# Attention and mixture of experts in one kernel: the weighting of a step in one piece, and the second half of the next batch's projections due earlier

## The chip, the cores and the metric

The kernel runs on one core of a Trainium2 chip. The metric is device time in microseconds (us) for one launch that does everything, from loading the inputs to storing the output. The core has five engines that each run their own list of instructions in order: the matrix engine (TensorE, PE in the profile), VectorE (DVE), ScalarE (ACT), GpSimd (POOL) and SyncE (SP, which issues most DMAs). They wait for each other by semaphores.

## The reference, cut to what matters

The input `x` has 8 batches of 1024 tokens with 256 features. All data is float32.

```python
x = x + layernorm(attention(layernorm(x)))   # 16 heads of 16 features, causal
x = x + layernorm(moe(layernorm(x)))         # 8 experts, 2 chosen per token

# attention, per batch and head
score = where(causal, q @ k.T / sqrt(16), -inf)
out   = softmax(score) @ v
# moe, per token
gate = min(x @ Wg[e] + bg[e], 7);  up = clip(x @ Wu[e] + bu[e], -7, 7)
y[e] = ((up + 1) * gate * sigmoid(1.702 * gate)) @ Wd[e] + bd[e]
out  = sum over the two best experts of softmax(x @ Wr.T + br)[e] * y[e]
```

## The kernel before

**Two stages.** First comes attention with everything around it, down to the choice of experts for every token; then the expert stage, which works through 71 tiles of 256 tokens of one expert each (`quarter`, L1265 to L1286, and `lower_half`, L1296 to L1306) and puts the outputs back in order (`both`). Between the two, the tokens go through HBM: each token's normalized row is scattered to its two experts' regions by indirect DMAs on the POOL queue (`xsd`, L1044).

**Units.** Attention is cut into 32 units: 8 batches times 4 groups of 4 heads (`b`, `g`). In a unit the four heads lie in the four groups of 32 partitions, so that four small matmuls (32 rows each) run at once, each on its quarter of the rows of the matrix engine. A unit is done in two passes. The first pass (`maxima_tiles`) computes all scores and keeps each query's maximum (`sa`, L686; the maxima on DVE at L696, L702, L711 and L740). The second pass (`values_tiles`), one unit behind, computes the transposed scores once more, this time with the maximum subtracted through an extra row (`sb`, L781), takes their exponentials on ACT (`pT`, L789), masks the diagonal blocks on POOL (L798), and multiplies them with the values (`av`, L818, called the weighting here; it uses the matrix engine as four groups of 32 columns). The row of maxima gets to its place by `rows`: a small reduction (`nm`, L652), a transpose (`nmps`, L655), a copy, and four DMAs on the SP queue (L659).

**Steps and pairs.** A unit has 9 steps. Six hold one row of 512 scores per head (kinds EDGE and WHOLE); three (kind TWO) hold two shorter pieces. A step is done in two pairs: pair 0 computes the scores of heads 0 and 1 of the first pass together with those of heads 2 and 3 of the second pass of the unit before, pair 1 the other way round. Each pair is one group of matmuls with all four row groups at work. The weighting runs two steps late (`DELAY = 2`). After the scores of a pair comes one half of the weighting of step k-2 (`f(kk, half)`), that is 256 of the 512 columns, and then the background (`pump`). In one step of each unit (k = 4, which weights step 2) the two halves belong to two blocks of queries, one of which ends as the other begins: half 0 completes the first block, which DVE must copy out of the single accumulator (`avs`, L829; pool `ps_v`, one buffer) before half 1 can start on the second.

**The background.** Everything else in the attention stage is a list of jobs that are Python generators cut into pieces, each with an estimated cost in us on PE, DVE, ACT and POOL. There are three classes: `urgent` (maxima rows, normalizing of finished rows, masked edges), `due` (the next batch: `prep` normalizes and transposes it, `xps`, L436; `project(b, 0)` and `project(b, 1)` make queries and keys of the first and of the last two units, `pjq` and `pjk`, L591; `values` makes v, `vps`, L577), of which only the first in line may run, and `back` (what follows a finished batch: `finish` with the output projection `aps`, L869, and `yps`, L877, the layer norm and residual; then `route` with the logits, the choice of experts, the slots and the scatters: `x2ps`, L935, `lpsT`, L942, `lps`, L950, `cps`, L996). `pump` adds credit for each engine (at most 0.9 us, 1.3 on POOL) and emits pieces as long as no engine that the piece uses has negative credit. A pair gives PE 0.68 us of credit. The engines' order in attention is exactly this order of emission, for PE, DVE, ACT and SP; POOL's is tied to it by extra dependencies (`in_order`). Jobs of class `back` go on being emitted in the first expert tiles.

**Due times before.** `project(b+1, 0)` is started in the third unit of batch b. `values(b+1)` and `project(b+1, 1)` are started at step 7 of the fourth unit, and forced to an end at the start of the second unit of batch b+1.

**Accumulators.** The scores `sa` have two buffers of two banks each. The scores `sb` and every background matmul share one pool, `ps_b`, of three buffers of one bank, taken in turn; a pair of the second pass takes two of them, each background job at least one. A buffer is free again when ACT or DVE has read it.

Of the kernel before, what the change touches and what calls it, by code (L numbers as in the profile page):

```python
# [58 lines left out]
def attn_moe_kernel(  # L59
# [345 lines left out]
    with ExitStack() as attn:  # L405
# [453 lines left out]

        def finish(b, c):  # L860

            last = b == B - 1
            a = a_toks.pop((b, c)).rearrange("p n h d -> p n (h d)")
            aT = ap2.tile([P, KT, QC], F32, tag="aT", name=f"aT_{b}_{c}")
            for kt in range(KT):
                yield piece(pe=0.5, act=0.6, after=0 if kt else 1)
                ps = ps_b.tile([P, NTB, P], F32, tag="b", name=f"aps_{b}_{c}_{kt}")
                for n in range(NTB):
                    nc.tensor.transpose(ps[:, n, :], a[:, n, ts(kt, P)], ident)  # L869
                nc.scalar.copy(aT[:, kt, :], ps.rearrange("p n q -> p (n q)"))  # L870
            y = ap2.tile([P, NTB, D], F32, tag="y", name=f"y_{b}_{c}")
# [27 lines left out]
            yield from route(b * NC + c, y, last)  # L899
# [18 lines left out]
        def route(t, x1, last):  # L918

            xn = ap2.tile([P, NTB, D + 1], F32, tag="xn2", name=f"xn2_{t}")  # L920
            if last:
                yield from normed(xn, x1)
            else:
                mv, rstd = yield from ln_steps(x1, NTB)
                for n in range(NTB):
                    yield piece(pool=1.25)
                    ln_apply(xn[:, n, :D], x1[:, n, :], mv, rstd, n, nc.gpsimd)

# [149 lines left out]
        def pump(*us):  # L1078

            nonlocal now  # L1080
            for i, more in enumerate(us):
                credit[i] = min(credit[i] + more, 1.3 if i == 3 else 0.9)
            found = True
            while found:
                found = False
                for kind, job in candidates():
                    if job.ready <= now and all(
                        not cost or has >= 0 for cost, has in zip(job.cost, credit)
                    ):
                        for i, cost in enumerate(job.cost):  # L1090
                            credit[i] -= cost
                        emit(kind, job)
                        found = True
                        break
            now += 1

# [21 lines left out]
        with tc.manual_schedule(  # L1118
# [11 lines left out]
            second, late = None, deque()  # L1130
            for u in range(B * NG + 1):
                first = None
                if u < B * NG:
                    b, g = divmod(u, NG)
                    if g == 1:
                        finish_by(jobs["v"], jobs["p1"])
                        if b + 1 < B:
                            jobs["x"] = start(due, prep(b + 1))
                    if g < NG - 1:
                        spread(u + 1)  # L1140
                    if b + 1 < B and g == 2:
                        jobs["p0"] = start(due, project(b + 1, 0))
                    first = maxima_tiles(u)
                for k in range(K):
# [4 lines left out]
                    if first and g == NG - 1 and b + 1 < B and k == K - 2:  # L1149
                        finish_by(jobs["p0"])  # L1150
                        spread(u + 1)
                        jobs["v"] = start(due, values(b + 1))
                        jobs["p1"] = start(due, project(b + 1, 1))
                    for pair in range(2):
# [16 lines left out]
                        halves = (pair,) if first else (0, 1)  # L1171
                        if len(late) > DELAY - 1 or (late and not second):
                            f, kk = late[0]
                            for half in halves:
                                f(kk, half)
                            if 1 in halves:
                                late.popleft()
                        if 1 in halves:
# [5 lines left out]
                        if first and second:  # L1184

                            us = 1.64 + 0.62
                            of_dve = {WHOLE: 1.22, EDGE: 1.68, TWO: 0.72}[STEPS[k][0]]
                            of_act = 1.8 if STEPS[k][0] == TWO else 1.2
                            pump(0.68, us - of_dve, us - of_act, us - 0.35)
# [288 lines left out]
```

## Time and profile before

| what | value |
|---|---|
| time, median of 3 runs | 2270.49 us (2268.22 to 2275.01) |
| profiled execution: its own time, its span | 2275.28 us, 2273.4 us |
| busy: PE, PE's weight loads, DVE | 2195.0, 1363.7, 1627.3 us |
| busy: ACT, POOL | 1091.8, 1070.1 us |
| last weighting of attention | ends about 1435 us |
| first to last expert matmul (L1265) | 1437.1 to 2243.9 us |
| scores `sb`, `sa`: instructions, mean | 3072 of 522 ns, 3072 of 526 ns |
| weighting `av`: instructions, mean | 5120 of 368 ns |

The page counts an engine busy while any instruction of it is under way. Matmuls overlap, and a float32 matmul stands in the profile as two records, so that busy PE time is not the sum of the means. A block of matmuls is best measured from its start to the start of the next block.

### The profile page before, as it was taken

What the parts mean: (1) busy time and instruction counts of PE and PEld (TensorE: products, weight loads), DVE (VectorE), ACT (ScalarE), POOL (GpSimd) and SP (SyncE); (2) the same over time, 40 slices, a digit from 0 to 9 for tenths busy, and PEclk for the clock granted to TensorE, in tenths of its full rate; (3) what the DMA queues carried; (4) which work ended last, traced back from release to release, by engine and by line L of the source; (5) the groups of instructions that cost most, each with busy time, mean ns of one, the idle gap of its engine ahead of it and who ended that gap; (6) DMA issues with size and microseconds to landing.
All of it is one profiled execution on the core that took longest, in us unless ns stands there. A gap on an engine that the chain in (4) does not pass through costs nothing.

```text
span 2273.4 us, 45180 instructions
## 1 busy us (share of the span) xinstructions
PE 2195.0 (97%) x16801; PEld 1363.7 (60%) x16801; DVE 1627.3 (72%) x3677; ACT 1091.8 (48%) x2181; POOL 1070.1 (47%) x1228
## 2 busy tenths in 40 slices
PE   7999999999999999999999999889999999999995
PEld 3444544444444444444445444677888888888884
DVE  4765777777777777777687686665557888887775
ACT  2565665665665666666656656431122323322222
POOL 3321463474364365365365354454444544554543
PEclk9999999999999999999999999999999999999998
DMA  3101102112012013012012010657667877878773
GB/s 81 39 2 39 21 21 58 28 32 58 12 39 48 21 30 86 12 33 55 21 29 58 21 39 30 230 179 221 202 216 256 281 256 268 269 248 279 244 249 110
DMA packets 149106, 251.05 MB, mean 110 GB/s; under 512 B 25920, under 2 KB 111832, under 8 KB 146840
## 3 DMA queue, kind: packets, MB, share of 16 engines
q1 hardware_dynamic: 134168, 210.86, 30.0%
q0 software_dynamic: 12960, 35.47, 4.3%
q8 instruction: 133, 2.18, 0.4%
q10 hardware_dynamic: 1760, 1.84, 0.3%
q14 instruction: 85, 0.70, 0.1%
HBM read 175.66 MB, written 55.68 MB: 102 GB/s over the span
## 4 chain that ended last, share of the span: by engine, by line
PE 83%; DVE 7%; POOL 4%; issue 3%; ACT 1%; DMA 1%; ACTq 0%; POOLq 0%; DVEq 0%; SPq 0%
PE sa L686 19%; PE gu L1265 18%; PE av L818 12%; PE dn L1296 10%; PE sb L781 8%; PE vps L577 3%; PE pjq L591 3%; PE pjk L591 3%; PE yps L877 3%; PE avt L849 1%; PE xtps L1249 1%; POOL pT L798 1%; DVE mx L702 1%; DVE mx L740 1%; DVE sa L696 1%
## 5 line engine op out<-in xcount | busy, mean ns | idle before, releaser
L789 ACT ACTIVATE pT<-sb 128x512 f32<-128x512 f32 x1152 | 625.1, 595 | 348.0 <-PE sb L781 316.8
L781 PE MATMUL sb<-qP,kP 32*128 32x512 f32 (+3 forms) x3072 | 720.0, 522 | 0.5 <-ACT pT L789 0.2
L686 PE MATMUL sa<-kP,qP 32*128 32x512 f32 (+3 forms) x3072 | 657.0, 526 | 6.2 <-DVE mx L702 3.0
L1265 PE MATMUL gu<-xsT,wg 128*128 128x256 f32 x2272 | 520.7, 382 | 2.5 <-ACT xsT L1251 2.5
L1265 PEld LDWEIGHTS gu<-xsT,wg 128*128 128x128 f32 x2272 | 433.9, 191 | 62.8 <-ACT xsT L1251 2.8
L798 POOL TENSOR_SCALAR_AFFINE_SELECT pT<-pT 128x512 f32<-128x512 f32 x256 | 160.3, 642 | 552.8 <-ACT pT L789 368.2
L702 DVE TENSOR_REDUCE mx<-sa 128x2 f32<-128x1024 f32 x256 | 311.5, 1219 | 140.9 <-PE sb L781 137.9
L1276 ACT ACTIVATE sig<-gate 128x256 f32<-128x256 f32 x284 | 118.3, 416 | 569.1 <-DVE gate L1274 540.2
L818 PE MATMUL av<-pT,vpad 128*32 128x256 f32 (+1 forms) x5120 | 366.2, 368 | 1.4 <-DVE avs L829 0.9
L686 PEld LDWEIGHTS sa<-kP,qP 32*128 32x128 f32 x3072 | 229.2, 184 | 207.8 <-issue 133.1
L1281 POOL TENSOR_TENSOR sig<-sig,gate 128x256 f32<-128x256 f32 x284 | 213.4, 753 | 279.8 <-ACT sig L1276 277.7
L781 PEld LDWEIGHTS sb<-qP,kP 32*128 32x128 f32 x3072 | 319.5, 184 | 30.0 <-ACT pT L789 4.6
L818 PEld LDWEIGHTS av<-pT,vpad 128*32 128x32 f32 x5120 | 106.1, 108 | 325.5 <-issue 277.1
L1296 PE MATMUL dn<-wd,act 128*128 128x256 f32 x1136 | 276.2, 384 | 14.1 <-DVE act L1286 14.1
L1274 DVE TENSOR_SCALAR gate<-gu,bs 128x256 f32<-128x256 f32 x284 | 136.0, 479 | 171.6 <-PE gu L1265 156.4
L1296 PEld LDWEIGHTS dn<-wd,act 128*128 128x128 f32 x1136 | 210.8, 192 | 46.5 <-DVE act L1286 21.0
L696 DVE CUSTOM_DVE_ANT_0 sa<-sa,cmask 128x512 f32<-128x512 f32 x256 | 178.3, 696 | 84.4 <-PE sb L781 62.3
L1306 POOL DMA_INDIRECT ytd<-ys,places x142 | 142.6, 1004 | 124.1 <-DVE ys L1302 96.5
L1044 POOL DMA_INDIRECT xsd<-xn,slots x128 | 128.2, 1002 | 107.2 <-DVE xn L1034 46.0
L711 DVE TENSOR_REDUCE mx<-sa 128x2 f32<-128x512 f32 x128 | 88.0, 687 | 88.4 <-PE sb L781 66.1
L1286 DVE SCALAR_TENSOR_TENSOR act<-up,sig 128x256 f32<-128x256 f32 x284 | 124.1, 437 | 21.4 <-POOL sig L1281 21.4
L1278 DVE TENSOR_SCALAR up<-gu,bs 128x256 f32<-128x256 f32 x284 | 134.6, 474 | 0.0
(198 smaller groups left out, 2390.3 us busy)
## 6 DMA issues: line engine op xcount, KB each, us to landing
wg<-_L_ffn_gate_up_proj_dram SPq DMA_DIRECT2D x71, 1024.0 KB
wd<-in_L_ffn_down_proj_dram SPq DMA_DIRECT2D x71, 512.0 KB
xs<-xsd SPq DMA_DIRECT2D x67, 257.0 KB
yy<-ytd SPq DMA_DIRECT2D x16, 1024.0 KB
bs<-biasd SPq DMA_DIRECT2D x71, 132.0 KB
x<-in_L_attn_x_dram SPq DMA_DIRECT2D x16, 512.0 KB
qP<-unq SPq DMA_DIRECT2D x128, 64.0 KB
x1d<-y SPq DMA_DIRECT2D x16, 512.0 KB
```

The source lines that it names most:

```text
L591: nc.tensor.matmul(ps, lhsT=wT[name][:, kt, ts(g2, P)], rhs=xnTs[b][:, kt, ts(c, QC)], start=(kt == 0), stop=(kt == KT - 1),)
L686: nc.tensor.matmul(ps[:, hh, ds(at, w)], lhsT=qP[r, ts(i, P)], rhs=kP[r, ds(c * QC, w)], start=True, stop=True,)
L696: nc.vector.tensor_tensor_reduce(out=ps[:, hh, :], in0=ps[:, hh, :], in1=cmask, scale=1.0, scalar=NEG, op0=ALU.add, op1=ALU.max, accum_out ...
L702: nc.vector.tensor_reduce(mx[:, heads, i, 2:3], ps, AX.X, ALU.max)
L781: nc.tensor.matmul(banks[hh][:, ds(at, QC - off)], lhsT=kP[r, ts(j, P)], rhs=qP[r, ds(c * QC + off, QC - off)], start=True, stop=True,)
L789: nc.scalar.activation(pT[:, 2 * pair + hh, :], banks[hh], AF.Exp)
L798: in_order(nc.gpsimd.affine_select(out=d, in_=d, compare_op=ALU.is_ge, fill=0.0, base=0, pattern=[[0, HG], [1, P]], channel_multiplier=-1,))
L818: nc.tensor.matmul(av[ds(hh * HS, HS), ds(off + a - at, z - a)], lhsT=vp[:, j, ds((g * HG + hh) * VS, HS)], rhs=pT[:, hh, a:z],  start=c n ...
L1265: nc.tensor.matmul(ps[:, half, :], lhsT=wg[:, kt, ds(half * FF + f * P, P)], rhs=xT[:, kt, :], start=(kt == 0), stop=(kt == KT - 1),)
L1281: in_order(nc.gpsimd.tensor_tensor(sg, sg, gt, ALU.mult))
L1296: nc.tensor.matmul(ps[:, n, :], lhsT=act[:, f, ts(n, P)], rhs=wd[:, f, :], start=(f == 0), stop=(f == FT - 1),)
L1306: put = nc.gpsimd.indirect_dma_start(out=yt_dram[:, :], out_offset=bass.IndirectOffsetOnAxis(ap=places[:, i, n : n + 1], axis=0), in_=y[:, ...
```

## The change

A step of attention is emitted as: the scores of pair 0; the background, with the whole step's PE credit (1.36 us); the scores of pair 1; and then the weighting as a whole. Where the background of the step gave less than 1.0 us of PE work, or where the weighted step belongs to two blocks of queries, half 0 of the weighting stays in the middle, now behind the background. At the end of the step a second `pump` adds no PE credit and takes only pieces with at most 0.2 us of PE work. `pump` returns the PE cost that it emitted.

`values(b+1)` and `project(b+1, 1)` are started at the beginning of the fourth unit of batch b instead of at its step 7.

The `finish` and `route` jobs of a block of 512 tokens are held back by a new generator `until`: the output projection of a block waits until the block two before it has its normalized rows for routing, and its routing waits until the block two before it has been routed.

```diff
+        def until(nth, far):
+            while nth >= 0 and gone[nth] < far:
+                yield piece(after=1)
         def finish(b, c):
+            nth = len(gone)
+            gone.append(0)
...
+            yield from until(nth - 2, 1)
             y = ap2.tile([P, NTB, D], F32, tag="y", name=f"y_{b}_{c}")
...
             nc.sync.dma_start(out=x1_dram[b * NC + c], in_=y)
-            yield from route(b * NC + c, y, last)
+            yield from until(nth - 2, 2)
+            yield from route(b * NC + c, y, last, nth)
+            gone[nth] = 2
...
+            gone[nth_job] = 1
...
-        def pump(*us):
+        def pump(*us, most=9.0):
...
-                    if job.ready <= now and all(
+                    if job.ready <= now and job.cost[0] <= most and all(
                         not cost or has >= 0 for cost, has in zip(job.cost, credit)
                     ):
+                        got += job.cost[0]
...
+                    if b + 1 < B and g == NG - 1:
+                        jobs["v"] = start(due, values(b + 1))
+                        jobs["p1"] = start(due, project(b + 1, 1))
...
                         finish_by(jobs["p0"])
                         spread(u + 1)
-                        jobs["v"] = start(due, values(b + 1))
-                        jobs["p1"] = start(due, project(b + 1, 1))
...
-                        halves = (pair,) if first else (0, 1)
+                        us = 1.64 + 0.62
+                        of_dve = {WHOLE: 1.22, EDGE: 1.68, TWO: 0.72}[STEPS[k][0]]
+                        of_act = 1.8 if STEPS[k][0] == TWO else 1.2
+                        left = us - of_dve, us - of_act, us - 0.35
+                        middle = first and pair == 0
+                        got = pump(1.36, *left) if middle and second else 0.0
                         if len(late) > DELAY - 1 or (late and not second):
                             f, kk = late[0]
+                            if middle:
+                                apart_of = len({t[0] for t in STEPS[kk][2]}) > 1
+                                halves = (0,) if got < 1.0 or apart_of else ()
+                                begun_with = halves
+                            else:
+                                halves = tuple(
+                                    h for h in range(2) if not (first and h in begun_with)
+                                )
                             for half in halves:
                                 f(kk, half)
-                            if 1 in halves:
+                            if not middle:
                                 late.popleft()
...
                         if first and second:
-                            us = 1.64 + 0.62
-                            of_dve = {WHOLE: 1.22, EDGE: 1.68, TWO: 0.72}[STEPS[k][0]]
-                            of_act = 1.8 if STEPS[k][0] == TWO else 1.2
-                            pump(0.68, us - of_dve, us - of_act, us - 0.35)
+                            if not middle:
+                                pump(0.0, *left, most=0.2)
```

More of the change, by code (lines that the diff above doesn't have):

```diff
@@ L858, in normalize @@
                 start(back, finish(b, c))
+        gone = []
+        def until(nth, far):
+            while nth >= 0 and gone[nth] < far:
+                yield piece(after=1)
         def finish(b, c):
+            nth = len(gone)
+            gone.append(0)
             last = b == B - 1
@@ L916, in normed, with route @@
             yield piece(after=1)
-        def route(t, x1, last):
+        def route(t, x1, last, nth_job):
             xn = ap2.tile([P, NTB, D + 1], F32, tag="xn2", name=f"xn2_{t}")
@@ L1076, in candidates @@
                     yield (due if kind is not urgent and kind is not back else kind), job
-        def pump(*us):
+        def pump(*us, most=9.0):
             nonlocal now
+            got = 0.0
             for i, more in enumerate(us):
@@ L1095, in pump @@
             now += 1
+            return got
         def finish_by(*jobs):
@@ L1129, in attn_moe_kernel @@
             jobs["p1"] = start(due, project(0, 1))
-            second, late = None, deque()
+            second, late, begun_with = None, deque(), ()
             for u in range(B * NG + 1):
@@ L1170, in attn_moe_kernel @@
                             use()
-                        halves = (pair,) if first else (0, 1)
+                        us = 1.64 + 0.62
[4 more added lines that the diff above has]
+                        got = pump(1.36, *left) if middle and second else 0.0
                         if len(late) > DELAY - 1 or (late and not second):
                             f, kk = late[0]
+                            if middle:
[6 more added lines that the diff above has]
+                                )
                             for half in halves:
                                 f(kk, half)
-                            if 1 in halves:
+                            if not middle:
                                 late.popleft()
-                        if 1 in halves:
+                        if not middle:
                             if first:
@@ L1184, in attn_moe_kernel @@
                         if first and second:
-                            us = 1.64 + 0.62
-                            of_dve = {WHOLE: 1.22, EDGE: 1.68, TWO: 0.72}[STEPS[k][0]]
-                            of_act = 1.8 if STEPS[k][0] == TWO else 1.2
-                            pump(0.68, us - of_dve, us - of_act, us - 0.35)
+                            if not middle:
+                                pump(0.0, *left, most=0.2)
                         elif first:
```

## The prediction

> **What bounds the kernel now.** I read the page's slices first, then the chain that ended last by engine, then PE's timeline. From the page:
>
> ```profile
> PE 2195.0 (97%) x16801; PEld 1363.7 (60%) x16801; DVE 1627.3 (72%) x3677; ACT 1091.8 (48%) x2181; POOL 1070.1 (47%) x1228
> ...
> PE   7999999999999999999999999889999999999995
> ...
> PE 83%; DVE 7%; POOL 4%; issue 3%; ACT 1%; DMA 1%; ACTq 0%; POOLq 0%; DVEq 0%; SPq 0%
> ```
>
> PE carries 83% of the chain and is busy almost throughout, also in attention (slices 2 to 25). That doesn't say that it works at its peak. The timeline of PE shows how its time is made up (start, duration, line, tile, shape, count):
>
> ```profile
> 616.00 0.66 PE L869 MATMUL aps<-ident,atok 128*128 128x128 f32 x4
> 616.58 0.70 PE L686 MATMUL sa<-kP,qP 32*128 32x512 f32 x2
> ...
> 617.65 0.64 PE L818 MATMUL av<-pT,vpad 128*32 128x256 f32 x8
> 618.22 1.99 PE L877 MATMUL yps<-woT,aT 128*128 128x256 f32 x8
> 620.15 0.70 PE L686 MATMUL sa<-kP,qP 32*128 32x512 f32 x2
> ```
>
> From start to start: a pair's scores (S) 1.07 us, half a weighting (A) 0.57, an output projection 1.93. Two halves in a row occur in the last unit:
>
> ```profile
> 1430.06 1.07 PE L818 MATMUL av<-pT,vpad 128*32 128x256 f32 x16
> 1431.06 1.99 PE L877 MATMUL yps<-woT,aT 128*128 128x256 f32 x8
> 1432.98 1.94 PE L818 MATMUL av<-pT,vpad 128*32 128x256 f32 x32
> ```
>
> They take 1.00 us, not 2 x 0.57: each change of kind costs about 0.14 us behind an A. A background block (B) before an A costs the same 1.92 as before S. Scores with background right behind them, as the changed order has them, stand in the first unit:
>
> ```profile
> 58.40 1.13 PE L686 MATMUL sa<-kP,qP 32*128 32x512 f32 x4
> 59.46 1.98 PE L591 MATMUL pjk<-xnT,wkT 128*128 128x512 f32 x4
> ```
>
> 1.06 us, so that order has no price of its own. I cut PE's timeline from 80 to 1425 us into S, A and B blocks. Above their shortest forms, about 100 us are waits: 79 inside S (for the `sb` buffers, mostly), the rest behind A and B.
>
> **What the Trainium skill says.** "TensorEngine Tiling (Array Packing)", Key Properties: changing the tiling mode drains the TensorE, changing the tile within a mode doesn't. The trace agrees: 0.57 + 0.57 against 1.00. "Perfetto Trace Analysis", Identifying the Most-Contended Engine: matmul busy time is no measure of headroom, weight loads are a better one. It agrees: in attention the loads are busy 75 to 77 of each 160 us while matmuls show 159. "PSUM — Partial Sum Buffer", Specifications: eight banks. The pools take 4 + 3 + 1, so the three `ps_b` buffers can't simply be more; the waits in S are its sign in the trace.
>
> **The change, part by part.** The built order of the changed kernel, between first and last weighting, against that of before: S 562 and 562; A blocks 564 and 418; B blocks 284 and 233. So 155 steps have their weighting whole; the others keep a half in the middle.
>
> 1. *Fewer drains at A*: 146 x 0.14 = 20.4 us gained.
>
> 2. *Fewer drains at B*: a normalizing transpose and a key projection together take 2.30, apart 0.59 + 1.91 = 2.50; two transposes together 1.02, apart 1.17. So 51 x 0.17 = 8.7 gained.
>
> 3. *Scores behind half a weighting alone.* Before, 275 S come 0.57 us after the last S and wait 0.15 on average (41 in total): the third `ps_b` buffer is free, the next one only when the exponential (0.595) of the last pair is read, 0.72 after its scores. After the change 181 are left, 27 us; the 148 S behind a whole weighting have 1.00 us of cover and should wait for nothing. Gain 14.
>
> 4. *Lost cover.* With no A in the middle, S1 comes right behind B. With one background job it needs both exponentials, about 1.22 us (a single transpose job, 1.17 after S, waits 0.05). With two, B's first job holds the buffer that S1 wants, and ACT reads it behind the exponentials. The chain of waits before shows it with an A as cover:
>
> ```profile
> 317.31 0.57 PE av L818 x8
> 317.88 1.02 PE x2ps L935 x8
> 318.90 0.63 PE sa L686 x2
> ...
> 320.26 0.57 PE av L818 x8
> ```
>
> S lasts 1.36, 0.29 over; so two jobs need 1.9 after S (2.1 in TWO steps, where ACT also copies edges, 0.59). Projections (1.92) and longer need no cover. But 43 packs of two or three short jobs, about 1.0 us long, just reach the 1.0 that moves A away: 43 x 0.9 = 39 us. B followed by A (78) keeps its cover, 21. Sum 60 against 44 by the same rule before (the trace has 53): 16 lost.
>
> 5. *The step that is split between two blocks.* DVE's copy `avs` (0.69) was queued right behind the first maxima; now up to 1.5 us of background pieces stand ahead of it on DVE, and only one S (1.07) lies between its two halves. Half 1 queues behind it on PE, and everything else behind that. From the order, in about nine of 31 units such pieces meet no or short background: 0.9 to 1.2 us each, 8 lost. Bounds 0 and 20.
>
> 6. *The earlier due time* adds and removes nothing: the same matmuls and ACT copies, no DMA, spread over two units instead of one; no lump at a forced end stood in the order before, so I take 0. Its cover is the slack of ACT (62% busy here); without it, seven batches' 56 copies x 0.59 = 33 us of ACT would meet the exponentials, as they do now.
>
> 7. *The hold-back and the tail.* Back jobs get PE credit only once per step and wait for each other. In the built order one routing more (block 13: `x2ps` 8 matmuls, `lpsT` 8, `lps` 1; 1.8 us of PE, moved, not saved) falls into the expert stage. Its layer norm (4 x 1.23 on POOL) stands in front of the gate products (L1281) there; its scatters were in that stage before as well. Windows there:
>
> ```profile
> 1435.00:1480.00 45.00, 36.25 (x166) 30.52 (x167) 32.80 (x105) 16.13 (x32) 25.32 (x28) 0.92 0.76 265
> 1480.00:1520.00 40.00, 37.44 (x215) 31.26 (x214) 31.23 (x110) 15.95 (x31) 23.09 (x26) 1.00 0.55 187
> 1520.00:1560.00 40.00, 32.58 (x127) 26.41 (x126) 18.89 (x55) 4.69 (x11) 20.31 (x23) 0.83 0.69 200
> ```
>
> PE (second figure) is not full: the first eight expert tiles take 122.6 us, against 10.8 each later, 36 over. An added exponential there swaps ACT's tables twice (1.28 each, as the trace has them). I take 5 lost, bounds 0 and 15. The second expert table is now emitted in tile 9 instead of 7; tile 12 needs it, two tiles (21.6 us) later, so loads stay covered.
>
> Sum: -20.4 - 8.7 - 14 + 16 + 8 + 5 = -14 us. Against the profiled execution's 2275.3 that is 2261; that one lies 4.8 above the median of the runs, so I forecast 2256 for the median.
>
> **Rivals.** (a) *The tail takes it*: three routings in the thin stage between the two instead of two and a bit; at 36 us for what is there, a third at 12 and a later table bring the gain to about nothing, 2268. For it: POOL waits and scatters on the chain there. Against: they are now spread over ten tiles, not eight. (b) *The lost cover decides* (slower): place, S1 behind 86 packs of two or three jobs without an A. I take 0 for the long ones and 0.9 for the short. If ACT or DVE reads a pack's first job late also there (edge copies, a DVE queue with 1.2 us maxima), by 0.55 each, that is 47 us: 2303; it turns the sign from 14/86 = 0.16 us on. A nearer value is 2285. Against: before, long packs (2.89 us behind S) waited 0.0 to 0.1. (c) *More gain*: items 4, 5 and 7 cost nothing, since S1 is late only where S0' would have been: -29 - 14 = -43, 2227; half of that, 2238, is likelier. (d) That it isn't done in full: true for 126 steps and already counted.
>
> **How the numbers follow.** My forecast 0.50 (2244 to 2264), (a) 0.20 (2262 to 2276), (b) 0.14 (2278 to 2303), (c) 0.16 (2227 to 2244). 0.3% is 6.8 us, about what a measurement can tell from no change: below 2263.7 lie nearly all of the forecast, (c) and a little of (a), 0.67; within, 0.19; above 2277.3, 0.14. The range 2234 to 2279 leaves out half of (c) and most of (b); the likeliest case's own is 2244 to 2264.
>
> **What would show it.** Right: `av` blocks of 16 records at 1.00 us, about 155 of them; S behind them at 1.07; S behind packs of two short jobs at 1.9 to 2.0; attention ending 15 to 25 us earlier; the first ten expert tiles 5 us longer in sum. Wrong: waits of S behind projections (b), or `avs` waits over 1 us in every unit; expert tiles 0 to 9 more than 15 us longer (a); fewer waits inside S in total than the 79 us of before (c).

## The result, and the profile after

| | before | after |
|---|---|---|
| time, median of the runs (us) | 2272.75 (2268.2 to 2277.9) | 2342.95 (2335.8 to 2348.0) |
| ratio | 1 | 1.0306, interval 1.0269 to 1.0343 |
| span of the profiled execution | 2273.4 | 2342.4 |
| first expert matmul | 1437.1 | 1464.5 |
| the first ten expert tiles together | 144.2 | 185.7 |
| from the eleventh tile to the start of the last | 652.5 | 652.5 |

The forecast was 2256 with a range of 2234 to 2279. The kernel became 70 us slower, and the loss has two places: 27.4 us in attention and 41.5 us in the first ten expert tiles. Together they are the 69.0 us by which the spans differ.

From the page after (busy times, PE by slice, the chain by engine):

```profile
PE 2188.7 (93%) x16801; PEld 1360.2 (58%) x16801; DVE 1631.4 (70%) x3677; ACT 1090.9 (47%) x2183; POOL 1071.0 (46%) x1228
...
PE   7999999999999999999999989776999999999995
...
PE 81%; DVE 6%; POOL 4%; ACT 4%; issue 4%; DMA 2%; ACTq 0%; POOLq 0%; SPq 0%; DVEq 0%
```

PE is busy for 6.3 us less, with the same 16801 matmul records, and the span is 69 us longer. The hole in the slices has grown from "889" to "89776". That is the tail; the 27 us in attention don't show here, since a slice of 58 us is still a "9" with 1 us more of waiting in it.

The windows of the tail after (columns: stretch, its length, then busy time and instruction count of PE, PEld, DVE, ACT and POOL, PE's granted clock, DMA share, GB/s):

```profile
1465.00:1510.00 45.00, 31.82 (x154) 24.77 (x153) 18.04 (x55) 13.81 (x26) 21.54 (x22) 0.85 0.57 195
1510.00:1550.00 40.00, 27.73 (x121) 22.72 (x120) 20.77 (x71) 9.10 (x20) 20.43 (x23) 0.83 0.51 164
1550.00:1590.00 40.00, 34.35 (x170) 28.77 (x173) 26.61 (x85) 11.83 (x24) 15.42 (x18) 0.87 0.39 132
```

PE, DVE and POOL all do less than in the same stage before, where PE had 36 of 45 and 37 of 40 us. No engine is full, so they wait for each other or for a transfer.

**Attention, cut into blocks.** PE's timeline between the first weighting and the last, cut as in the prediction into scores (S), weightings (A) and background (B): "shortest form" is what the blocks would take at the durations that the prediction used, "above it" is the rest.

| us | before: shortest form | above it | after: shortest form | above it |
|---|---|---|---|---|
| S | 601.3 | 79.0 | 601.3 | 84.3 |
| A | 326.6 | 15.2 | 306.2 | 7.0 |
| B | 322.9 | 10.5 | 312.8 | **71.2** |

The saved changes of kind are there in number: 30.5 us at the prediction's prices. What takes them, and 27 more, is 61 us of waits inside background. By the number of jobs (each fills one `ps_b` buffer) in a block that stands right behind scores:

| jobs in the block | blocks | wait inside, each | sum |
|---|---|---|---|
| 1 | 109 | 0.02 us | 2.0 us |
| 2 | 98 | 0.53 us | 52.0 us |
| 3 | 17 | 0.92 us | 15.6 us |

One of them in the timeline after (start, duration, engine, line, what, and in brackets how long the engine had been idle and who ended that):

```profile
659.16 0.59 PE L686 MATMUL sa<-kP,qP 32*128 32x512 f32 x2
659.18 0.59 PE L781 MATMUL sb<-qP,kP 32*128 32x512 f32 x2
...
659.70 0.28 PE L655 MATMUL nmps<-ident,nm 128*16 128x128 f32 x1
...
659.93 1.09 ACT L789 ACTIVATE pT<-sb 128x512 f32<-128x512 f32 x2 [0.80 <-PE sb L781]
...
660.58 0.65 PE L849 MATMUL avt<-ident,avs 128*128 128x128 f32 x4 [0.60 <-ACT pT L789]
660.90 0.24 ACT L657 COPY nmT<-nmps 16x128 f32<-16x128 f32 x1
...
661.07 1.98 PE L591 MATMUL pjk<-xnT,wkT 128*128 128x512 f32 x4
...
662.98 0.70 PE L686 MATMUL sa<-kP,qP 32*128 32x512 f32 x2
```

The pair's scores have taken two of the three `ps_b` buffers, and `nmps`, the pack's first job, takes the third. The second job, `avt`, has to take over the buffer that the first exponential reads. That exponential begins at 659.93, takes 0.60, and `avt` starts at 660.58. The third job, `pjk`, gets the buffer of the second exponential, which is read until 661.02, and starts at 661.07. That is 0.49 us behind `avt`, a distance that it also has in e5 below with half a weighting ahead, so nearly all of the loss lies in front of the second job. The pack takes 3.28 us; its shortest forms add up to 2.36. Before the change half a weighting (0.57 us) stood between scores and pack, and most of the first exponential's time passed under it. In the list of PE's waits of attention before, background waits for the exponentials come to 1.0 us; after, the list begins with

```profile
PE avt L849 <- ACT pT L789: 9.9, 20, 0.6
PE x2ps L947 <- ACT pT L789: 7.6, 18, 0.6
PE yps L886 <- ACT pT L789: 5.5, 14, 0.5
```

(us in all, times, longest), and so on through twelve kinds of job; the weight loads (PEld) show more of the same.

**The tail.** POOL's waits from 1430 to 1660 us, the row that has changed, first of before, then of after (us in all, times, longest):

```profile
POOL xsd L1044 <- DMA xn<-second: 11.0, 2, 6.8
```

```profile
POOL xsd L1056 <- DMA xn<-second: 35.7, 4, 12.1
```

`xsd` are the scatters; those for a token's second expert need new row numbers in the rows' last column, and a small DMA on SP's queue writes these (`xn<-second`). The last of the four waits, in the timeline after:

```profile
1620.08 0.37 SPq L1259 DMA_DIRECT2D wg<-_L_ffn_gate_up_proj_dram  x1
...
1621.24 0.37 SPq L1267 DMA_DIRECT2D wd<-in_L_ffn_down_proj_dram  x1
...
1623.45 0.61 SPq L1052 DMA_DIRECT2D xn<-second  x1
...
1637.08 0.96 POOL L1056 DMA_INDIRECT xsd<-xn,slots  x1 [12.06 <-DMA xn<-second]
...
1639.33 0.73 POOL L1311 TENSOR_TENSOR sig<-sig,gate 128x256 f32<-128x256 f32 x1
1640.09 0.42 DVE L1316 SCALAR_TENSOR_TENSOR act<-up,sig 128x256 f32<-128x256 f32 x1 [14.72 <-POOL sig L1311]
...
1640.57 1.22 PE L1326 MATMUL dn<-wd,act 128*128 128x256 f32 x2 [13.37 <-DVE act L1316]
```

The write of 2 KB is issued 3.4 us behind an expert's 1 MB and 2.2 us behind its 512 KB. POOL stands at the scatter until 1637. The gate product `sig` is queued behind the scatters, DVE stands at `act` for 14.7 us, and PE at `dn` for 13.4. (In this last of the four, ACT had itself been held by another DMA until 1632.9; POOL's wait outlasts that by 4 us.)

Why the write comes late is not the same each time. The four writes were ready 5.9, 2.8, 7.6 and 13.6 us after their issue; in the first two cases POOL had stood for 3.5 and 4.0 us before the write was issued at all, and seven DMAs of zeros (257 KB each, L262) are issued 1.7 us behind the last one. Whether the bulk loads ahead of it hold the write back was not tested.

One remark on the numbers below: the kernel before takes 2274 us on the chip of the runs e1 to e4, but 2291 and 2292 on the two chips of e5 to e8 and e9 to e12, where attention with the order of before is some 25 us longer (1461.9 against 1437.1 for the first expert matmul; two single waits inside scores of 4.0 and 4.8 us are part of it). Times are therefore set against the kernel before on the same chip, and attention against a kernel with the same order on the same chip; the forecasts of the first expert matmul for e5 to e12, made from 1437 and 1464, have to be read in this way. e1 to e9 are one execution each. The first scores start between 25.9 and 32.7 us, before any of the edits can act, and shift the first expert matmul with them; so the table also has the time from the first weighting to the last.

### The profile page after: what moved, and what is told of

It reads as the page before. It is cut to its first block, busy times and chain, and to the rows that moved or that the text cites. A ratio compares the mean times of both kernels' runs of the same rounds, so it can differ in the third digit from the quotient of the medians.

```text
span 2342.4 us, 45151 instructions
## 1 busy us (share of the span) xinstructions
PE 2188.7 (93%) x16801; PEld 1360.2 (58%) x16801; DVE 1631.4 (70%) x3677; ACT 1090.9 (47%) x2183; POOL 1071.0 (46%) x1228
## 3 DMA queue, kind: packets, MB, share of 16 engines
q1 hardware_dynamic: 134168, 210.86, 29.2%
## 4 chain that ended last, share of the span: by engine, by line
PE 81%; DVE 6%; POOL 4%; ACT 4%; issue 4%; DMA 2%; ACTq 0%; POOLq 0%; SPq 0%; DVEq 0%
PE sa L686 20%; PE gu L1295 18%; PE av L818 11%; PE dn L1326 9%; PE sb L781 7%; ACT pT L789 3%; PE vps L577 3%; PE pjk L591 3%; PE pjq L591 3%; PE yps L886 2%; PE xtps L1279 1%; POOL xsd L1056 1%; PE avt L849 1%; PE x2ps L947 1%; DMA xn<-second 1%
## 5 line engine op out<-in xcount | busy, mean ns | idle before, releaser
L781 PE MATMUL sb<-qP,kP 32*128 32x512 f32 (+3 forms) x3072 | 710.3, 523 | 1.9 <-ACT pT L789 1.0
L818 PE MATMUL av<-pT,vpad 128*32 128x256 f32 (+1 forms) x5120 | 336.6, 366 | 5.0 <-DVE avs L829 5.0
L781 PEld LDWEIGHTS sb<-qP,kP 32*128 32x128 f32 x3072 | 293.7, 184 | 43.2 <-ACT pT L789 6.7
L1326 PE MATMUL dn<-wd,act 128*128 128x256 f32 x1136 | 276.6, 384 | 32.7 <-DVE act L1316 32.7
L818 PEld LDWEIGHTS av<-pT,vpad 128*32 128x32 f32 x5120 | 121.1, 109 | 238.5 <-issue 176.4
```

Source lines behind the costliest of these rows:

```text
L781: nc.tensor.matmul(banks[hh][:, ds(at, QC - off)], lhsT=kP[r, ts(j, P)], rhs=qP[r, ds(c * QC + off, QC - off)], start=True, stop=True,)
L818: nc.tensor.matmul(av[ds(hh * HS, HS), ds(off + a - at, z - a)], lhsT=vp[:, j, ds((g * HG + hh) * VS, HS)], rhs=pT[:, hh, a:z],  start=c n ...
L1326: nc.tensor.matmul(ps[:, n, :], lhsT=act[:, f, ts(n, P)], rhs=wd[:, f, :], start=(f == 0), stop=(f == FT - 1),)
```

## The experiments

The theories at the start. **Theory 1**: attention loses because the second and third job right behind scores wait for the buffers that the exponentials read. Its rivals: the larger lumps of background cost by themselves, or the earlier due time does. **Theory 2**: the tail loses because one more block is routed there, and its scatters wait for late writes. Its rivals: the order of the step spoils the tail itself, or the routing's own work fills it.

All runs in one table (us; "second scatters" is the sum of POOL's waits for `xn<-second` in the expert stage):

| kernel | first expert matmul | first to last weighting | waits in S | in B | ten tiles | second scatters | time | before, same chip |
|---|---|---|---|---|---|---|---|---|
| before | 1437.1 | 1352.8 | 79 | 11 | 144.2 | 11.0 | 2272.8 | |
| after | 1464.5 | 1380.1 | 84 | 71 | 185.7 | 35.7 | 2343.0 | 2272.8 |
| e1 old order, due + hold | 1454.6 | 1370.2 | 99 | 12 | 137.7 | 5.0 | 2286.2 | 2274.3 |
| e2 new order alone | 1478.3 | 1393.6 | 99 | 68 | 141.9 | 11.0 | 2313.8 | 2274.3 |
| e3 new order + hold | 1474.6 | 1389.4 | 99 | 66 | 155.3 | 15.5 | 2323.9 | 2274.3 |
| e4 before, swapped | 1480.9 | 1394.5 | 95 | 52 | 158.1 | 5.7 | 2332.6 | 2274.3 |
| e5 before, lumps behind half 0 | 1469.8 | 1390.5 | 128 | 15 | 141.5 | 11.7 | 2304.9 | 2290.9 |
| e6 after, one job behind scores | 1461.3 | 1381.3 | 118 | 4 | 186.0 | 36.7 | 2341.3 | 2290.9 |
| e7 after, late scatters | 1488.2 | 1403.1 | 107 | 69 | 141.7 | 3.8 | 2323.0 | 2290.9 |
| e8 before, late scatters | 1461.9 | 1373.9 | 97 | 13 | 138.4 | 0 | 2293.9 | 2290.9 |
| e9 after, half exponentials | 1439.9 | 1356.9 | 75 | 49 | 185.3 | 31.5 | 2319.1 | 2291.8 |
| e10 = e6 + e7 | 1458.4 | 1378.2 | 117 | 3 | 141.3 | 3.2 | 2297.0 | 2291.8 |
| e11 before, long single jobs ahead | 1453.3 | 1369.0 | 98 | 13 | 140.2 | 0 | 2284.0 | 2291.8 |
| e12 as e11, whole step's credit | 1466.1 | 1381.0 | 121 | 21 | 140.4 | 0 | 2297.8 | 2291.8 |

### Which part of the change loses (e1 to e3)

e1 takes the new order of the step out and keeps the rest:

```diff
-                        middle = first and pair == 0
-                        got = pump(1.36, *left) if middle and second else 0.0
+                        halves = (pair,) if first else (0, 1)
 ...
+                            pump(0.68, us - of_dve, us - of_act, us - 0.35)
```

> The order of the step undone (half, scores, half, background as before); the earlier due time and the hold-back stay. Theory 1 (background right behind the scores waits for the score buffers) expects the loss in attention gone: first expert matmul at 1437 +-5 us, as before. Theory 2 (the tail is lost to the routing of block 13, moved into the expert stage, and to the scatters there) expects the first ten expert tiles at 144 +-10 us, since only blocks 14 and 15 are routed there in this order; time about 2275. Rival: the earlier due time or the hold-back carry the loss; then this run lies 20 us or more over the kernel before.

Measured: 12 us over the kernel before; first expert matmul 17.5 us later, ten tiles 6.5 us shorter. Background waits are gone (12 us), as Theory 1 says. But attention is not back: waits inside scores grew from 79 to 99. So the earlier due time and the hold-back together are not free in this order, which neither theory had; the two were not taken apart here. The rival, 20 us or more in all, did not come either. By the unit's place in its batch (first to fourth, sums over eight batches), background in shortest form and waits inside scores:

| us | before: B, waits in S | e1: B, waits in S | e2: B, waits in S | after: B, waits in S |
|---|---|---|---|---|
| first units | 96, 17 | 85, 23 | 108, 15 | 73, 18 |
| second | 90, 18 | 56, 33 | 69, 40 | 74, 25 |
| third | 81, 19 | 75, 22 | 81, 17 | 73, 24 |
| fourth | 56, 25 | 108, 21 | 57, 27 | 93, 18 |

The early due time moves v and second projections into the fourth unit and leaves the second nearly bare, and there the waits of e1 are largest. In each pair of columns they are largest where the unit has least background, or nearly least. That is a pattern and no proof, and in the second units of e2 something else stands behind it. Of their 40 us, 12 are five single waits of 1.9 to 3.1 us, one in each batch from the third to the seventh, behind a pack of `avt` and `x2ps` or `aps`. One of them in e2's timeline:

```profile
598.67 0.65 PE L849 MATMUL avt<-ident,avs 128*128 128x128 f32 x4
...
599.53 0.66 PE L945 MATMUL x2ps<-ident,xn 128*128 128x128 f32 x4 [0.20 <-ACT pT L789]
...
601.52 0.42 DVE L853 TENSOR_TENSOR atok<-avt,rec 128x256 f32<-128x256 f32 x1
...
602.10 0.66 PE L781 MATMUL sb<-qP,kP 32*128 32x256 f32 x1 [1.28 <-DVE atok L853]
```

DVE reads `avt` only behind several small steps of the routing and a maximum, and the second `sb` of the next pair waits for that buffer. Before the change no wait inside scores is longer than 1.2 us.

e2 takes out the two other edits instead; e3 takes out only the earlier due time:

```diff
-            yield from until(nth - 2, 1)          # e2 only
-            yield from until(nth - 2, 2)          # e2 only
-                    if b + 1 < B and g == NG - 1:
-                        jobs["v"] = start(due, values(b + 1))
-                        jobs["p1"] = start(due, project(b + 1, 1))
 ...
                         spread(u + 1)
+                        jobs["v"] = start(due, values(b + 1))
+                        jobs["p1"] = start(due, project(b + 1, 1))
```

> The new order of the step alone, without the earlier due time and without the hold-back. Theory 1: attention as long as after the change or a little longer (in the built order 91 blocks of two and 21 of three jobs come right behind scores, against 98 and 17), first expert matmul at 1464 to 1470 us. Theory 2: routing of blocks 14 and 15 only in the expert stage, so its first ten tiles take 144 +-10 us and the time is about 2300. Rival to theory 2 (the order of the step spoils the tail itself): ten tiles at about 186 us, time about 2343. Rival to theory 1 (the earlier due time costs the attention's 27 us): first expert matmul at 1437 or before.

> The new order of the step with the hold-back, the earlier due time alone undone. Theory 1: attention as after the change, first expert matmul at 1464 +-5 us. Theory 2: block 13 is routed in the expert stage here too, so the ten tiles take 186 +-12 us and the time is about 2343. Rival (the earlier due time carries part of the loss): 15 us or more less than after the change.

Measured, adding one edit at a time:

| | attention | ten tiles |
|---|---|---|
| new order of the step (e2 less before) | +41.2 | -2.3 |
| hold-back (e3 less e2) | -3.7 | +13.4 |
| earlier due time (after less e3) | -10.1 | +30.4 |
| sum | +27.4 | +41.5 |

The order alone loses more in attention than I expected (1478, not 1464 to 1470): background waits as priced (68 against 48 + 19 = 67 by Theory 1's prices), and 20 us more inside scores than before the change. Nine waits of over 1.4 us make 18.5 of these 20, the five above among them. With the new order the earlier due time gives 10 us back: the five waits are gone (waits of over 1.4 us: 18.0 us in e3, 5.0 after). In e3 the five packs stand in step 2 of the second units, and DVE is done with `avt` 3.3 to 3.5 us after its start; after the change such packs stand in step 5 of the first units, DVE is done after 1.7 to 2.0 us, and the scores wait 0.6. So it has no sign of its own. The -2.3 and -3.7 of the table say nothing, since four executions of the kernel before differ by up to 9.7 us. The tail's part of Theory 2 was right for e2 (141.9). It missed for e3: block 13 is routed in the expert stage there too, and the ten tiles took 155, not 186 +-12. So the extra routing isn't the size of the loss. What goes with it is the column of second scatters: 11.0 us of waits in e2, 15.5 in e3, 35.7 after. Nor does one edit make the loss of the tail: in e1 the due time and the hold-back without the order leave 137.7 us. The new order with the earlier due time but without the hold-back was not run.

### Behind the scores, or lumps anywhere (e4 to e6)

e4 is the kernel before with the two statements of a pair exchanged: `pump` ahead of `f(kk, half)`. Every instruction of before is there, but part of the output comes out wrong in this order; why was not traced, and only the times of its attention are used.

> The kernel before with one edit: in each of a step's pairs the background is put ahead of the half weighting, so that it comes right behind the scores; no weighting is whole, no hold-back, the old due time. In the built order 194 background blocks of one job come right behind scores, 78 of two and 5 of three. Theory 1 prices them at 0, 0.53 and 0.92 us: 46 us lost, 6 saved by fewer and longer blocks; first expert matmul at about 1470 us. Rival (the loss comes from the whole weighting, or from uneven load on ACT and DVE, not from what stands behind the scores): at 1437 or a little before.

Measured: 1480.9, more than the 1470 expected; background waits 52 us, 0.51 in front of two jobs and 0.65 of three, against 0.53 and 0.92 priced, and 16 more inside scores. So no whole weighting and no lump of a whole step is needed for the waits; to stand right behind scores is enough.

e5 makes the lumps without putting them behind scores:

```diff
-                            pump(0.68, us - of_dve, us - of_act, us - 0.35)
+                            if pair:
+                                pump(0.0, *left, most=0.2)
+                            else:
+                                pump(1.36, *left)
```

> The kernel before with one edit: the whole step's background is given in the step's first pair, behind half 0 of the weighting (as in the kernel before, a weighting stands between the scores and it), and the second pair gets next to none. As large lumps as after the change (118 blocks of one job, 93 of two, 22 of three), but none right behind scores. Theory 1 (what counts is that the lumps stand right behind scores) expects no loss: first expert matmul at 1437 - 9 (fewer changes of kind) = 1428 +-6 us. Rival (the lumps themselves cost, wherever they stand): 1455 us or more. The tail at 144 +-15 us.

Measured: from the first weighting to the last 16.6 us longer than e8, whose attention is that of the kernel before on the same chip. (The first expert matmul is only 7.9 us later, because e5's first weighting starts 8.7 us sooner.) Theory 1 in this form wanted 9 less, the rival at least 18 more; both miss, the rival by little. The waits inside background stay away (15 us against e8's 13). The same three jobs as in the timeline above, here behind half a weighting:

```profile
646.85 0.64 PE L818 MATMUL av<-pT,vpad 128*32 128x256 f32 x8
647.42 0.28 PE L655 MATMUL nmps<-ident,nm 128*16 128x128 f32 x1
647.63 0.66 PE L849 MATMUL avt<-ident,avs 128*128 128x128 f32 x4
648.12 1.98 PE L591 MATMUL pjk<-xnT,wkT 128*128 128x512 f32 x4
650.03 0.70 PE L686 MATMUL sa<-kP,qP 32*128 32x512 f32 x2
```

From `nmps` to the next scores 2.61 us, against 3.28. But the lumps do cost, in another place: scores behind them wait 66.7 us (232 times) against 49.6 (283 times) in e8, and those with only half a weighting ahead 61.7 (329) against 47.6 (279), 31 us more inside scores in all. The mean behind lumps, 0.29 us, is not the price of every lump: the median is below 0.01. Fifteen waits of over 1.4 us make 31.6 us of the total, against four and 12.0 in e8; five of them (11.4 us) stand behind `avt` with `x2ps` or `aps` as in e2 above, four (10.7 us) behind `lpsT`. So there are two prices: one inside a pack that stands right behind scores, paid by nearly every such pack, and one in the next scores for a step's background in one lump, paid mostly in a few places that come back with each batch.

e6 is the changed kernel with at most one PE job behind the scores; more of them go behind half 0:

```diff
-                        got = pump(1.36, *left) if middle and second else 0.0
+                        got = pump(1.36, *left, jobs=1, tick=0) if middle and second else 0.0
 ...
-                                halves = (0,) if got < 1.0 or apart_of else ()
+                                halves = (0,) if got < 1.0 or apart_of or more_to_do() else ()
 ...
+                        if middle and second:
+                            pump(0.0, 0.0, 0.0, 0.0)
```

> The changed kernel with one edit: at most one PE job goes right behind the scores; where more are due, half 0 of the weighting follows it and the others stand behind that (224 blocks of one job right behind scores, none of two or three; built nominal length 1252 against 1220). Theory 1: waits inside background 0.02 each instead of 0.53 and 0.92, so 67 us less waiting against 32 us more changes of kind: first expert matmul at 1437 +-8 us. Rival (the waits come from the load on ACT and DVE and only move): 1464 us or later, the waits then inside the scores. The tail as after the change, 186 +-15 us.

Measured, from the first weighting to the last: 21.8 us less than e7, which has the changed kernel's attention on the same chip, and 7.4 more than e8. (The first expert matmul flatters e6 by the 5.0 and 7.9 us that its first weighting starts sooner.) Between e8 and e7 lie 29.2 us, so three quarters of the loss in attention are gone. Background waits fall by 64 us, scores wait 11 more, and 32 us of changes of kind come back: the sum is -21 by the blocks. The 7.4 that remain are 21 us more inside scores than in e8 against 14.5 less in weightings. The tail is unchanged at 186, as expected.

### The second scatters (e7 and e8)

```diff
-                    yield piece(after=(2 if last else 1))
+                    yield piece(after=(8 if t >= NT - LATE else 1))
```

> The changed kernel with one edit: for the last four blocks the second expert's scatters are emitted eight ticks of the background pump behind the write of their row numbers, instead of one or two, so that POOL's queue goes on with gate products while that write is on its way. Attention as after the change (1464 +-4 us). Theory 2 (POOL stands at the second scatter for that write, 36 us in all in the expert stage, and the gate products behind it stop DVE and PE): ten tiles 20 to 35 us shorter than 186 us. Rival (the routing's own work on PE, DVE and POOL fills the stage): within 8 us of 186.

> The same edit on the kernel before. Attention at 1437 +-3 us. Its trace shows 11 us of waits at the second scatter in the expert stage (4.2 and 6.8), so Theory 2 expects ten tiles of 144 - 11 = 133 +-6 us and a time of about 2263. Rival: 144 +-4 us, no change.

Measured: ten tiles 141.7 in e7, 44 less than after the change and than e6 on the same chip, more than the 20 to 35 expected and all of the tail's loss; 138.4 in e8, 5.8 less than before and 3.1 less than e5 on the same chip (133 +-6 was expected). e8's forecast of 11 us less in all did not come: one execution took 2293.9 us against 2290.9 for one of the kernel before, and single executions can't tell a few us (46 of the kernel before on the chip of e9 to e12 lie between 2286 and 2303). What is left of the four waits in e7, from POOL's list of waits of the stage (us, times, longest):

```profile
POOL xsd L1056 <- DMA xn<-second: 3.8, 1, 3.8
```

And from PE's list, the wait for `act`, after the change and in e7:

```profile
PE dn L1326 <- DVE act L1316: 29.3, 6, 13.4
```

```profile
PE dn L1326 <- DVE act L1316: 2.9, 3, 1.5
```

Block 13 is routed in the expert stage in e7 too. So it is the wait that costs and not the work, and Theory 2 stands in that narrower form. The 24.7 us of such waits more than before come with 41.5 us of time. One part of the rest is on record: after the change the granted clock of PE was 0.83 to 0.87 in all four windows of the ten tiles (1465 to 1650 us), in e7 1.00, 0.87, 1.00 and 1.00 (1488 to 1630), and PE was busy for 135.6 us there against 126.1. The lower clock goes along with the waits; how the rest comes about was not taken apart. e4's 158 us with only 5.7 us of such waits is not explained by this and stays open.

### The wait measured by its cause (e9)

```diff
-                        nc.scalar.activation(pT[:, 2 * pair + hh, :], banks[hh], AF.Exp)
+                        nc.scalar.activation(
+                            pT[:, 2 * pair + hh, : QC // 2], banks[hh][:, : QC // 2], AF.Exp
+                        )
```

> The changed kernel with exponentials of half the columns (128x256; POOL fills the other half of each weighting tile with ones, so the attention's values are not the reference's); the order on PE is unchanged. An activation of 128x256 takes 0.42 us in the gate's row, one of 128x512 0.60: 0.18 less. Theory 1 (the second job right behind the scores waits for the end of the first exponential, the third for that of the second) expects 0.53 - 0.18 = 0.35 us in front of two jobs and 0.92 - 0.36 = 0.56 in front of three: 44 us instead of 68 in all inside the background. Rival (the wait is the background's own: its inputs, its own reads by ACT and DVE, or changes of kind): 0.53 and 0.92 as before.

Measured: 0.37 us in front of two jobs (98 blocks) and 0.58 in front of three (17), 47 us in all. The exponential's end sets the wait in front of the second job: 0.16 us less where its time is 0.18 less. The rival is out. The 0.58 for three jobs agrees with 0.56 in the sum but not in the parts: in `nmps`, `avt`, `pjk` (seven times) the second job starts 0.66 us behind the first instead of 0.88, and the third 0.49 behind the second in both kernels. So the second exponential is at most a small part of the 0.92.

### Both causes, and what is left as gain (e10 to e12)

> Both suspected causes taken out of the changed kernel together: one PE job at most right behind scores (as in the kernel with cover), and the late second scatters. Theory 1 and Theory 2 together expect attention at 1437 +-8 us and ten tiles at 141 +-6 us, that is the time of the kernel before, 0.997 to 1.005 of it. Rival (a third cause): over 1.008.

Measured: 1.0025 of the kernel before, interval 1.0015 to 1.0035. The two edits bring 3.1% down to a quarter of a per cent; no third cause of size is left in the sum. It is a sum, though: scores still wait 117 us, and fewer changes of kind pay for that.

e11 is the kernel before, with the late scatters, and with a long job alone ahead of half 0:

```diff
+                        long_one = middle and second and next_is_long(*spare)
+                        if long_one:
+                            pump(*spare)
 ...
+                                begun_with = (0,) if not long_one or apart_of else ()
 ...
-                            pump(0.68, us - of_dve, us - of_act, us - 0.35)
+                            if not long_one:
+                                pump(*spare)
```

> The kernel before with what the runs left as gain: in a step's first pair, where the next PE job is a long one (1.0 us or more), it stands alone ahead of half 0, and the weighting follows whole behind the second scores; everywhere else the order and the credit of each pair are those of before; the late second scatters added. In the built order 34 weightings are whole and 41 single jobs stand right behind scores. Theory 1: 34 x 0.14 = 4.7 us gained, no new waits inside the background; Theory 2: ten tiles at 138 instead of 144. Sum -11: 0.993 to 0.998 of the kernel before. Rival (any background right behind scores costs more than it saves): 1.000 or above.

Measured: 0.9967 of the kernel before, interval 0.9952 to 0.9982, faster than both kernels. Its blocks against e8's (on another chip): waits inside scores 98 and 97, inside background 13 and 13, weightings 336.7 us against 342.2. The 5.5 us are the 34 changes of kind (4.7 expected); the 41 jobs right behind scores wait 0.03 us each.

e12 does the same with the whole step's credit in the first pair (`pump(0.0, *left)` behind a credit of 1.36).

> As the last, but with the changed kernel's credit: the step's whole background in its first pair, ahead of half 0 if its first PE job is a long one, behind it otherwise (60 blocks of one job and 6 of two right behind scores, 65 weightings whole, 233 blocks in all; built nominal length 1233 against 1250.8). Theory 1 in its first form: 18 us gained, 3 lost, attention at 1422 us. What the kernel with lumps behind half 0 showed (waits inside scores of 0.29 us each behind lumps, about 25 us in all) says the gain is eaten: 1437 +-8 us. Ten tiles at 138 +-5 us; time 0.990 of before by the first, 0.996 to 1.001 by the second.

Measured: 1.0022 of the kernel before, interval 1.0010 to 1.0034, just above the second forecast and far from the first. Scores behind background wait 0.29 us on average (231 times, 67 us), the figure of e5, and as there it is made in a few places: waits of over 1.4 us inside scores are 18 with 33.4 us, against 4 with 14.2 in e11, and these 19 us are most of the 23 that e12's scores wait longer. What the long jobs gain is lost there.

## Why the prediction was wrong

**Steps 1 and 2, fewer changes of kind: right.** 29.1 forecast, 30.5 by the number of blocks in the trace (A 20.4, B 10.1), at the same prices. The price for A holds when measured on its own: 5.5 us for 34 in e11.

**Step 3, scores behind half a weighting alone: wrong in size.** A gain of 14 was forecast. The 148 scores behind a whole weighting wait 0.03 each, as it said; but the 182 others wait 0.22 instead of 0.15, so that all together wait 45 us against 41 before. There is no gain. Why the others wait longer was not tested.

**Step 4, lost cover: this is the step that failed in attention.** It asked how long the scores *behind* a pack wait: nothing behind the 43 long packs, 39 us behind the 43 short ones. The long ones came as said (2 us), the short ones cost 16. It did not ask how long the pack itself waits, and said "Projections (1.92) and longer need no cover". They do not cover their own start: `avt` + `pjq` takes 2.77 us behind scores where 1.92 and 0.4 were due. 16 us of loss were forecast at the scores behind background, where 3 came (39 against 36); what came besides was 68 us inside packs, where the second job waits for the buffer that the first exponential reads. The evidence for the order was misread. The first-unit example (scores, then `pjk`, 1.06 us) was taken as a sign that this order "has no price of its own". But those scores are `sa` alone: no `sb` holds a `ps_b` buffer there, no exponential reads one, and a single job stands behind. And all packs of before that were looked at had half a weighting ahead of them, which is the cover whose price was asked for.

**Step 5, the split step: right in size.** 8 forecast; waits in the scores between its two halves grew by about 7.

**Step 6, earlier due time at 0: wrong, with no sign of its own.** With the hold-back 17.5 us later in e1's order, alone 10.1 earlier in the changed one. The step counted matmuls and copies, which are the same, and not what stands next to what: in the changed order the earlier due time moves the packs of `avt` and `x2ps` or `aps`, which held up the scores in e3, to a step where DVE reads `avt` sooner. What it does in e1's order is open.

**Step 7, the tail: wrong by the largest amount.** 5 forecast, bounds 0 and 15; measured 41.5. The step counted the moved routing's work and said that "its scatters were in that stage before as well". It left out that each second scatter waits for a DMA on SP's queue and stops all of POOL's work behind it: 35.7 us of such waits against 11.0. With the late scatters the same routing costs nothing (e7).

**The rivals.** (b) had the right kind, "lost cover", and 0.55 us each; it put it in the scores behind the pack, and against it stood the long packs of before, which were covered. What it describes, DVE reading a pack's first job late, does occur in e2 and e3, but five times, for 12 us, and not after the change. That its 2303 is near what the order alone gives (2314 in e2) is therefore luck. (a) named POOL's waits in the tail, but with 12 us. Neither alone reaches 2343; both came together.

Of its own signs, the 155 whole weightings at 1.00 us and the scores at 1.07 behind them came as said. "S behind packs of two short jobs at 1.9 to 2.0" did not (short packs: 1.45 on average), nor did "attention ending 15 to 25 us earlier" and "5 us longer in sum". Of the signs of being wrong, the one for (a) came: expert tiles 0 to 9 more than 15 us longer.

## What to carry to other kernels

When work is moved, follow each buffer ring through the new order and ask when the *moved* instructions get their buffers, not only who waits behind them; a pattern taken as evidence must use the same buffers. On an in-order queue with indirect DMAs, price each instruction by the transfer that it waits for and by what is queued behind it, and find when that transfer is issued and what is issued around it. A mean can hide where a cost sits: one long job behind the scores gained and whole steps in a lump lost, but most of that loss came from fewer than twenty single waits, five of them for a buffer whose reader stood far back in its queue.

## What was unexpected

- A write of 128x4 floats, with 1.5 MB of loads issued just ahead of it and 1.8 MB of zeros just behind, held its reader until 13.6 us after its issue; another after the change, also behind 1.5 MB of loads, until 7.6 us; in e7 one issued ahead of the next tile's loads was ready after 6.5 us.
- The kernel before differs by 0.8% between chips (2274 against 2291 and 2292), more than some of the effects here.
- The wait in front of a second job follows the exponential: with exponentials shorter by 0.18 us it falls from 0.53 to 0.37 (0.35 worked out).
- Small jobs hold large things up: in e2 one DVE step of 0.42 us (`atok`) read its buffer late in five batches, and the scores lost 1.9 to 3.1 us each time.
